# A new written order for the side work of two state-space layers: 99 parts of a block, placed anew among its 16 steps

## The chip, the cores and the metric

The kernel runs on one core of a Trainium2 chip. The metric is device time in microseconds (us), the median of several executions. One execution is also recorded by the hardware profiler; its span, from the first to the last instruction, and its rows are what is read here.

## What is computed

The input x has 64 sequences of 64 tokens with 256 features, and each sequence has a condition vector of 512. Four layers are added to x in turn: two conditioned attention layers (L0, L1; 16 heads) and two state-space layers (L2, L3). The change touches only the state-space layers. Cut to what matters, one of them is:

```python
xr, gate = split(x @ W_in.T, 2)              # 512 + 512 features
xc = silu(conv(xr + t_emb, W_conv) + b_conv) # four taps along the sequence, each feature alone
xn = layernorm(xc) * ln_g + ln_b
Bm, Cm, dt = split(xn @ W_xproj.T, 3)        # 16 states
dt = tanh(dt @ W_dt.T + b_dt) * 0.01
Ad = 1 + dt * -tanh(A_log)
Bd = Bm * minimum(norm(xn), 1)
h  = clip(h * Ad + Bd * xn, -10, 10)         # one step; h is 16 x 512 for each sequence
y  = Cm . h + D * xn
x  = x + (y * silu(gate)) @ W_out.T
```

Everything is fp32.

## The kernel before

The attention layers come first. The two state-space layers are then cut into 16 **blocks** (`items`, L150): 2 layers x 2 groups of 32 sequences x 4 pieces of 16 tokens. A block has 16 **steps** of the recurrence, so there are 256 steps in a row, and a step works on all 32 sequences: 8 sequences x 16 states fill the 128 partitions, in four groups of 512 columns.

What makes up step i is written at the end of the kernel (L1064 to L1118), with a moment for each part:

- `clips(i)` at i: two instructions of VectorE (DVE), one for each half of the state, which add the scaled state `v` to the input products `pu`, bound the sum and write `h`.
- `scales(i+1, half)` at i + 0.2 and i + 0.3: four instructions of ScalarE (ACT), two for each half, `v` = `h` times the decay of the next step.
- `inputs(i+1)` at i + 0.5: four products of TensorE (PE) into `pu`, from the spread weights `bd` and the normalized `xn`. Each half of `pu` has one buffer, so a half is written only after its clip.
- `outputs` of two steps together, at the odd step + 0.6: eight products into `py`.

All other work of a block is **side work**: 99 parts, methods of `Block` (L153 to L515). In the order of a block they are: for each of four feature groups c, `project` (PE, the input projection), `collect` (ACT copies it, GpSimd, POOL, adds the condition), `begin` and three `tap`s (ACT, then DVE: the convolution), `silu` (ACT); for each of four token groups j, `turn_x` (PE transposes), `stats` (DVE, two small POOL operations, DVE), `norm` (POOL) and `length` (ACT); once, `shared`, `keep`, `flip`, `flipped`, `params`, `decay`, `spreads`, `turn_a`, `turned_a`, `turn_c`, `turned_c`, `strength`, `by_step` (the parameters of the recurrence); `spread_b` (POOL, the weights `bd` of four steps); `gate` (PE, two products for each c) and `open` (ACT); `skip` (POOL) and `take` (DVE: y from `py`); `turn_y` (PE) and `gated` (DVE); `leave` (PE, eight products of the output projection, accumulated for two halves oc) and `residual` (DVE; in the second layer also the stores on the SP queue).

Where each part goes is written out in a table, `plan` (L996 to L1028): a moment in steps, counted from the block's first step. A part at -34.951 of block n is issued 34.951 steps before block n starts, so among the steps of block n - 3. Moments of all blocks, and those of the steps, are sorted (L1116), and the parts are issued in that order. Each engine instruction is pinned to it (`pin`, L104), so each engine works its own instructions in exactly this order; it waits in front of the first one whose operands or buffers are not ready. Parts that the attention phase already did for blocks 0 to 2 are left out (`done`), the last block has an `ending` of its own (L1030), and five steps of preparation for the second layer's weights are put at 9.15 to 13.15 (L1053).

Buffers bear on it too. PSUM has eight banks here: two halves of `pu` with two banks each, one for `py`, one for `acc` (the projection), and two **side banks** (`side_bank`, L142) that all other products share: `turn_x`, `shared`, `flip`, `turn_a`, `turn_c`, the gates, `turn_y` and the two sums of `leave`. A gate's bank is held from its first product to `open`, a sum's from its first `leave` to its `residual`.

Of the kernel before, what the change touches and what calls it, by code (L numbers as in the profile page):

```python
# [60 lines left out]
def tile_kernel(ctx: ExitStack, tc: tile.TileContext, ins, out):  # L61
# [916 lines left out]
    with tc.tile_pool(name="m1", bufs=1) as m1, tc.tile_pool(  # L978
# [6 lines left out]
        for i in range(2):  # L985
# [8 lines left out]


        plan = [  # L996
            (-34.951, "project", 0), (-34.145, "collect", 0), (-32.918, "begin", 0),
            (-32.296, "tap", 0, 1), (-32.249, "tap", 0, 2), (-31.945, "tap", 0, 3),
            (-31.244, "silu", 0), (-30.886, "project", 1), (-29.870, "collect", 1),
            (-28.982, "begin", 1), (-28.108, "tap", 1, 1), (-28.033, "tap", 1, 2),  # L1000
            (-27.458, "tap", 1, 3), (-27.391, "silu", 1), (-27.108, "project", 2),
            (-25.727, "collect", 2), (-25.628, "begin", 2), (-24.258, "tap", 2, 1),
            (-24.257, "tap", 2, 2), (-23.560, "tap", 2, 3), (-23.559, "silu", 2),
            (-23.297, "project", 3), (-22.516, "collect", 3), (-21.680, "begin", 3),
            (-20.388, "tap", 3, 1), (-20.387, "tap", 3, 2), (-19.648, "tap", 3, 3),
            (-19.425, "silu", 3), (-18.608, "turn_x", 0), (-17.021, "stats", 0),
            (-14.414, "turn_x", 1), (-13.823, "stats", 1), (-13.037, "norm", 1),
            (-12.466, "length", 1), (-11.619, "turn_x", 2), (-10.326, "stats", 2),
            (-9.009, "shared"), (-8.837, "keep"), (-8.735, "flip"), (-8.734, "flipped"),
            (-8.314, "turn_x", 3), (-7.276, "norm", 0), (-7.023, "norm", 2), (-7.022, "length", 2),  # L1010
            (-6.528, "stats", 3), (-5.896, "length", 0), (-4.945, "norm", 3), (-4.663, "params"),
            (-3.934, "decay"), (-3.655, "spreads"), (-3.160, "turn_a"), (-2.843, "turned_a"),
            (-1.863, "length", 3), (-1.855, "strength"), (-1.854, "by_step"),
            (-1.719, "spread_b", 0), (-1.036, "gate", 0, 0), (-0.523, "gate", 0, 1),
            (-0.416, "spread_b", 2), (-0.078, "open", 0), (0.962, "turn_c"), (1.060, "turned_c"),
            (1.971, "spread_b", 1), (2.598, "gate", 1, 1), (2.842, "gate", 2, 0),
            (3.137, "gate", 1, 0), (3.278, "open", 1), (3.495, "skip", 0), (4.308, "take", 0),
            (4.595, "gate", 2, 1), (4.863, "open", 2), (5.711, "spread_b", 3), (7.365, "skip", 1),
            (8.657, "take", 1), (10.567, "skip", 3), (12.293, "skip", 2), (13.392, "take", 2),
            (14.025, "gate", 3, 1), (14.668, "gate", 3, 0), (15.371, "open", 3),  # L1020
            (16.062, "turn_y", 1), (16.607, "gated", 1), (16.957, "turn_y", 0),
            (17.151, "gated", 0), (17.536, "take", 3), (22.035, "turn_y", 3),
            (22.093, "turn_y", 2), (22.428, "gated", 3), (22.838, "gated", 2),
            (23.084, "leave", 0, 3), (24.583, "leave", 0, 2), (26.250, "leave", 1, 2),
            (27.268, "leave", 1, 1), (27.476, "leave", 1, 0), (27.494, "leave", 1, 3),
            (28.056, "leave", 0, 1), (28.309, "residual", 1), (28.898, "leave", 0, 0),
            (29.565, "residual", 0),
        ]  # L1028

        ending = [  # L1030
# [150 lines left out]
```

## Time and profile before

| | us |
|---|---|
| median of 3 runs | 1613.23 (1610.12 to 1615.07) |
| the profiled execution: time | 1610.09 |
| its span | 1608.3 |
| attention, up to the first clip of the scan | 0 to 579.1 |
| 256 steps, first clip's start to last clip's end | 579.1 to 1597.3 |
| a block of 16 steps, between blocks 2 and 12 | 63.6 to 63.9 |
| block 0, 13, 14 | 66.6, 62.2, 62.2 |

In the profile PE is TensorE, PEld its weight loads, DVE VectorE, ACT ScalarE, POOL GpSimd and SP the engine that issues the DMAs. A row of groups gives line, engine, operation, out<-in with shapes and count, then the busy time in us and the mean of one instruction in ns, then how long the engine stood idle before them and what ended that. A row of the timeline gives the start in us, the length, the engine, the operation and, in brackets, the idle time before it. An fp32 matmul appears as two instructions, so `pu` of one step counts x8. Its ends are modelled: successive rows overlap a little, and the distance from one start to the next says better how long something held the engine.

### The profile page before, as it was taken

To read this page: it belongs to the slowest core of one execution; us is meant where nothing else is said; L and a number is where in the kernel's file an instruction comes from. 1 tells how busy PE (TensorE), PEld (TensorE's weight loads), DVE (VectorE), ACT (ScalarE), POOL (GpSimd) and SP (SyncE) were. 2 spreads that over 40 slices of the span, in tenths; PEclk is the share of its full clock that TensorE was granted. 3 is DMA by queue.
4 is the path that set the end of the run, shared out by engine and by line. 5 is a ranking of instruction groups with operands and counts; after the bars stand their busy time and mean duration, and the time that the engine had idled before them with its cause. 6 is when DMAs were issued, how large, how long until landed. Compare 5 with 4: busy or idle time off the path is not lost. (4 is left out here: it accounts for less than half of the span.)

```text
span 1608.3 us, 30098 instructions
## 1 busy us (share of the span) xinstructions
PE 1525.1 (95%) x12352; PEld 661.3 (41%) x12352; DVE 1304.2 (81%) x1480; ACT 1122.1 (70%) x1899; POOL 868.6 (54%) x862
## 2 busy tenths in 40 slices
PE   5899999999999688999999999999999999999888
PEld 2555555555555333333333333333333333333323
DVE  3777677777767687989989989889899899898775
ACT  3555555455456477888878888888888887887774
POOL 2467666646667656455455464554564644645420
PEclk9999999999999889999999999999999999999999
DMA  7000000000000010000000000000000000000001
GB/s 240 2 2 2 2 2 1 2 2 2 1 2 2 1 64 1 1 1 1 1 1 1 1 1 1 0 1 1 1 1 14 14 1 14 14 1 14 9 5 27
DMA packets 19337, 18.26 MB, mean 11 GB/s; under 512 B 5472, under 2 KB 16352, under 8 KB 19200
## 3 DMA queue, kind: packets, MB, share of 16 engines
q1 hardware_dynamic: 19200, 16.34, 3.2%
q8 instruction: 98, 1.61, 0.4%
q14 instruction: 39, 0.32, 0.1%
HBM read 12.14 MB, written 4.19 MB: 10 GB/s over the span
## 5 line engine op out<-in xcount | busy, mean ns | idle before, releaser
L113 ACT ACTIVATE v<-h,ad 128x512 f32<-128x512 f32 x1008 | 649.6, 711 | 142.3 <-DVE h L1082 133.9
L1082 DVE CUSTOM_DVE_ANT_0 h<-v,pu 128x1024 f32<-128x1024 f32 x504 | 592.3, 1216 | 111.2 <-ACT v L113 51.5
L107 PE MATMUL pu<-xn,bd 32*128 32x512 f32 x2048 | 293.6, 641 | 35.0 <-DVE h L1082 31.3
L107 PE MATMUL py<-h,cd 128*32 128x512 f32 x2048 | 247.1, 600 | 0.1
L107 PE MATMUL pw<-xm,aw 128*128 128x512 f32 x384 | 179.6, 606 | 3.9 <-POOL xm L730 3.9
L206 POOL TENSOR_TENSOR xr<-xr,cT 128x512 f32<-128x512 f32 x55 | 70.6, 1283 | 194.6 <-ACT xr L205 194.6
L107 PEld LDWEIGHTS pu<-xn,bd 32*128 32x128 f32 x2048 | 83.3, 183 | 177.0 <-issue 139.8
L822 POOL TENSOR_TENSOR pr<-pr,sm 128x1024 f32<-128x1024 f32 x64 | 121.1, 1903 | 21.7 <-DVE sm L821 20.2
L306 POOL TENSOR_SCALAR mv<-mv 128x1 f32<-128x1 f32 x64 | 14.7, 230 | 214.2 <-DVE mv L304 212.9
L107 PE MATMUL pg<-xt,win 128*128 128x512 f32 x256 | 126.8, 617 | 0.0
L107 PE MATMUL pw<-z,wo 128*128 128x512 f32 x240 | 126.6, 630 | 0.0
L117 DVE SCALAR_TENSOR_TENSOR acc<-xr,cv,acc 128x512 f32<-128x512 f32 x165 | 123.8, 751 | 2.0
L107 PE MATMUL acc<-xt,win 128*128 128x512 f32 x256 | 124.4, 609 | 0.7 <-ACT xc L113 0.7
L107 PEld LDWEIGHTS py<-h,cd 128*32 128x32 f32 x2048 | 53.7, 109 | 165.6 <-issue 163.0
L836 ACT COPY pT<-pt 128x512 f32<-128x512 f32 x128 | 68.4, 586 | 76.1 <-PE pt L110 76.1
L113 ACT ACTIVATE pr<-pr 128x1024 f32<-128x1024 f32 x64 | 67.7, 1057 | 61.1 <-DVE pr L123 61.1
L107 PEld LDWEIGHTS pw<-xm,aw 128*128 128x128 f32 x384 | 68.9, 191 | 74.0 <-issue 65.3
L440 POOL TENSOR_TENSOR dx<-xn,rep 128x512 f32<-128x512 f32 x64 | 82.0, 1281 | 18.7 <-DVE ys L123 18.7
L718 POOL TENSOR_TENSOR sq<-sq 128x512 f32<-128x512 f32 x16 | 20.4, 1277 | 129.2 <-ACT sq L113 129.2
L811 DVE TENSOR_REDUCE mx<-ps 128x16 f32<-128x1024 f32 x64 | 78.3, 1223 | 13.7 <-PE ps L107 13.7
L323 POOL TENSOR_TENSOR xn<-xg,rep 128x512 f32<-128x512 f32 x64 | 81.7, 1277 | 8.0 <-ACT xg L113 3.3
L123 DVE TENSOR_TENSOR pr<-ps,mx 128x1024 f32<-128x1024 f32 x64 | 78.4, 1225 | 8.6 <-DVE mx L811 0.5
(150 smaller groups left out, 2324.9 us busy)
## 6 DMA issues: line engine op xcount, KB each, us to landing
xt<-in_xT SPq DMA_DIRECT2D x8, 512.0 KB, 7.8
out_xT<-xt SPq DMA_DIRECT2D x14, 256.0 KB, 2.3
aw<-in_aw SPq DMA_DIRECT2D x10, 256.0 KB, 6.3
win<-in_win SPq DMA_DIRECT2D x2, 1024.0 KB, 8.3
rep<-in_rep SPq DMA_DIRECT2D x2, 784.0 KB, 7.7
wo<-in_wo SPq DMA_DIRECT2D x2, 512.0 KB, 8.0
out_xT<-xt SPq DMA_DIRECT2D x2, 192.0 KB, 2.5
wx<-in_wx SPq DMA_DIRECT2D x2, 96.0 KB, 7.2
```

Source lines behind the costliest of these rows:

```text
L107: pin(nc.tensor.matmul(*args, **kw))
L113: pin(nc.scalar.activation(*args, **kw))
L117: nc.vector.scalar_tensor_tensor(out=out, in0=in0, scalar=scalar, in1=in1, op0=op0, op1=op1)
L123: pin(nc.vector.tensor_tensor(*args))
L206: pin(nc.gpsimd.tensor_tensor(curb, curb, bc(temb, 2, BT), ALU.add))
L323: pin(nc.gpsimd.tensor_tensor(self.xn[j], xg, self.rep[:, DI : 2 * DI], ALU.add))
L440: pin(nc.gpsimd.tensor_tensor(self.dx[j], self.xn[j], self.rep[:, 2 * DI : 3 * DI], ALU.mult))
L718: pin(nc.gpsimd.tensor_tensor(a, a, self.sq[:, 1, :], ALU.add))
L811: pin(nc.vector.tensor_reduce(mx, s4, AX.X, ALU.max))
L822: pin(nc.gpsimd.tensor_tensor(pr, pr, bc(sm, 3, S), ALU.mult))
L836: pin(nc.scalar.copy(self.pT[g][:, c, :, :], pt))
L1082: nc.vector._custom_dve(TENSOR_ADD_SAT, out=hn, in0=vs.pop((i, h)), in1=pu[h], s0=10.0, s1=-10.0)
```

## The change

Only the table `plan` is replaced; its 99 parts stay the same, and no other line differs. Moments move by up to some ten steps. Where two neighbouring parts keep their order between the parts of the steps, nothing changes on an engine; where they do not, its list changes.

```diff
         plan = [
-            (-34.951, "project", 0), (-34.145, "collect", 0), (-32.918, "begin", 0),
-            (-32.296, "tap", 0, 1), (-32.249, "tap", 0, 2), (-31.945, "tap", 0, 3),
-            (-31.244, "silu", 0), (-30.886, "project", 1), (-29.870, "collect", 1),
-            (-28.982, "begin", 1), (-28.108, "tap", 1, 1), (-28.033, "tap", 1, 2),
-            (-27.458, "tap", 1, 3), (-27.391, "silu", 1), (-27.108, "project", 2),
-            (-25.727, "collect", 2), (-25.628, "begin", 2), (-24.258, "tap", 2, 1),
-            (-24.257, "tap", 2, 2), (-23.560, "tap", 2, 3), (-23.559, "silu", 2),
-            (-23.297, "project", 3), (-22.516, "collect", 3), (-21.680, "begin", 3),
-            (-20.388, "tap", 3, 1), (-20.387, "tap", 3, 2), (-19.648, "tap", 3, 3),
-            (-19.425, "silu", 3), (-18.608, "turn_x", 0), (-17.021, "stats", 0),
-            (-14.414, "turn_x", 1), (-13.823, "stats", 1), (-13.037, "norm", 1),
-            (-12.466, "length", 1), (-11.619, "turn_x", 2), (-10.326, "stats", 2),
-            (-9.009, "shared"), (-8.837, "keep"), (-8.735, "flip"), (-8.734, "flipped"),
-            (-8.314, "turn_x", 3), (-7.276, "norm", 0), (-7.023, "norm", 2), (-7.022, "length", 2),
-            (-6.528, "stats", 3), (-5.896, "length", 0), (-4.945, "norm", 3), (-4.663, "params"),
-            (-3.934, "decay"), (-3.655, "spreads"), (-3.160, "turn_a"), (-2.843, "turned_a"),
-            (-1.863, "length", 3), (-1.855, "strength"), (-1.854, "by_step"),
-            (-1.719, "spread_b", 0), (-1.036, "gate", 0, 0), (-0.523, "gate", 0, 1),
-            (-0.416, "spread_b", 2), (-0.078, "open", 0), (0.962, "turn_c"), (1.060, "turned_c"),
-            (1.971, "spread_b", 1), (2.598, "gate", 1, 1), (2.842, "gate", 2, 0),
-            (3.137, "gate", 1, 0), (3.278, "open", 1), (3.495, "skip", 0), (4.308, "take", 0),
-            (4.595, "gate", 2, 1), (4.863, "open", 2), (5.711, "spread_b", 3), (7.365, "skip", 1),
-            (8.657, "take", 1), (10.567, "skip", 3), (12.293, "skip", 2), (13.392, "take", 2),
-            (14.025, "gate", 3, 1), (14.668, "gate", 3, 0), (15.371, "open", 3),
-            (16.062, "turn_y", 1), (16.607, "gated", 1), (16.957, "turn_y", 0),
-            (17.151, "gated", 0), (17.536, "take", 3), (22.035, "turn_y", 3),
-            (22.093, "turn_y", 2), (22.428, "gated", 3), (22.838, "gated", 2),
-            (23.084, "leave", 0, 3), (24.583, "leave", 0, 2), (26.250, "leave", 1, 2),
-            (27.268, "leave", 1, 1), (27.476, "leave", 1, 0), (27.494, "leave", 1, 3),
-            (28.056, "leave", 0, 1), (28.309, "residual", 1), (28.898, "leave", 0, 0),
-            (29.565, "residual", 0),
+            (-34.879, "project", 0), (-34.720, "collect", 0), (-34.633, "begin", 0),
+            (-33.762, "tap", 0, 1), (-32.894, "tap", 0, 2), (-32.566, "tap", 0, 3),
+            (-32.565, "silu", 0), (-31.236, "project", 1), (-30.916, "collect", 1),
+            (-30.065, "begin", 1), (-28.224, "tap", 1, 1), (-28.223, "tap", 1, 2),
+            (-27.735, "tap", 1, 3), (-27.425, "silu", 1), (-26.834, "project", 2),
+            (-26.461, "collect", 2), (-25.058, "begin", 2), (-24.473, "tap", 2, 1),
+            (-24.064, "tap", 2, 2), (-23.845, "tap", 2, 3), (-23.358, "silu", 2),
+            (-23.074, "project", 3), (-22.756, "collect", 3), (-22.104, "begin", 3),
+            (-21.929, "tap", 3, 1), (-20.282, "tap", 3, 2), (-19.380, "tap", 3, 3),
+            (-19.357, "silu", 3), (-18.968, "turn_x", 0), (-18.058, "stats", 0),
+            (-14.435, "turn_x", 1), (-13.645, "stats", 1), (-11.623, "turn_x", 2),
+            (-10.897, "norm", 0), (-10.812, "length", 0), (-10.053, "stats", 2),
+            (-10.052, "norm", 2), (-9.499, "shared"), (-8.665, "keep"), (-8.250, "turn_x", 3),
+            (-7.092, "length", 2), (-6.345, "stats", 3), (-5.989, "flip"), (-5.825, "flipped"),
+            (-5.824, "params"), (-5.686, "decay"), (-5.144, "spreads"), (-4.236, "turn_a"),
+            (-3.382, "norm", 3), (-3.306, "turned_a"), (-3.276, "norm", 1), (-2.841, "length", 3),
+            (-1.920, "length", 1), (-0.646, "strength"), (-0.637, "by_step"),
+            (-0.636, "spread_b", 0), (-0.636, "spread_b", 1), (-0.635, "gate", 0, 1),
+            (0.558, "turn_c"), (0.559, "turned_c"), (1.526, "gate", 0, 0), (2.256, "open", 0),
+            (2.853, "gate", 1, 1), (2.912, "skip", 0), (3.191, "gate", 2, 1),
+            (3.200, "gate", 1, 0), (3.213, "spread_b", 2), (3.639, "open", 1), (4.278, "take", 0),
+            (4.417, "spread_b", 3), (5.088, "gate", 2, 0), (5.088, "open", 2), (8.209, "skip", 1),
+            (8.511, "skip", 2), (8.597, "take", 1), (12.046, "skip", 3), (12.174, "take", 2),
+            (14.587, "gate", 3, 1), (14.790, "gate", 3, 0), (15.873, "open", 3),
+            (16.070, "turn_y", 1), (16.545, "gated", 1), (17.046, "take", 3),
+            (17.476, "turn_y", 0), (17.477, "gated", 0), (22.325, "turn_y", 2),
+            (22.326, "gated", 2), (22.364, "turn_y", 3), (22.381, "gated", 3),
+            (23.280, "leave", 0, 0), (24.804, "leave", 0, 3), (26.021, "leave", 0, 2),
+            (26.537, "leave", 0, 1), (26.574, "leave", 1, 2), (27.053, "leave", 1, 0),
+            (27.632, "residual", 0), (28.514, "leave", 1, 1), (29.637, "leave", 1, 3),
+            (30.996, "residual", 1),
         ]
```

Sorted by engine, and modulo 16 steps, the products of PE between the input products of step k and those of step k + 1 (a part with a moment from k - 0.5 to k + 0.5) differ as follows; even k also hold the outputs of two steps:

| k | before | after |
|---|---|---|
| 1 | turn_y 0, turn_c, project 1 | turn_c, project 1, turn_y 0 |
| 2 | turn_x 1 | gate (0,0), turn_x 1 |
| 7 | shared, leave, flip | shared, leave |
| 10 | leave | flip, leave |
| 12 | leave | turn_a |
| 13 | turn_a, leave, project 0, turn_x 0 | leave, turn_x 0, project 0 |
| 14 | gate (3,1) | leave |
| 15 | gates (3,0), (0,0), (0,1) | gates (3,1), (3,0), (0,1) |

The other k hold the same kinds and numbers of products before and after.

## Prediction

> **What bounds the kernel now.** I read the page's busy shares and groups first, then the busy time by stage, then the timeline of the tensor engine. The page: busiest is PE, and the two costliest groups are the scales on ACT and the clips on DVE, each of which waits for the other and for the input products `pu`.
>
> ```profile
> PE 1525.1 (95%) x12352; PEld 661.3 (41%) x12352; DVE 1304.2 (81%) x1480; ACT 1122.1 (70%) x1899; POOL 868.6 (54%) x862
> L1082 DVE CUSTOM_DVE_ANT_0 h<-v,pu 128x1024 f32<-128x1024 f32 x504 | 592.3, 1216 | 111.2 <-ACT v L113 51.5 <-PE pu L107 49.8 <-issue 3.2
> L107 PE MATMUL pu<-xn,bd 32*128 32x512 f32 x2048 | 293.6, 641 | 35.0 <-DVE h L1082 31.3 <-DVE h L1079 2.9 <-ACT ad L113 0.4
> ```
>
> Busy time by stage, for a stretch inside the state-space steps (length, then PE, PEld, DVE, ACT, POOL busy): PE is at 98, DVE at 92, ACT at 85.
>
> ```profile
> 900.00:1000.00 100.00, 97.82 (x592) 35.94 (x588) 92.04 (x106) 84.61 (x147) 48.68 (x57) 1.00 0.00 1
> ```
>
> So a step has a floor, and PE fills most steps to it. The floor is seen late in the scan, where little else runs (timeline of all engines):
>
> ```profile
> 1561.60 2.35 DVE L1082 CUSTOM_DVE_ANT_0 h<-v,pu 128x1024 f32<-128x1024 f32 x2 [0.37 <-ACT v L113]
> ...
> 1564.10 1.14 PE L107 MATMUL pu<-xn,bd 32*128 32x512 f32 x8 [1.62 <-DVE h L1082]
> ...
> 1565.41 1.22 DVE L1082 CUSTOM_DVE_ANT_0 h<-v,pu 128x1024 f32<-128x1024 f32 x1 [1.46 <-ACT v L113]
> ```
>
> Two clips 2.35, 0.15 until the next input products may overwrite their banks, 1.14 for these, 0.17 to the next clip: 3.81 to 3.83 us. I call what PE does between the input products of step k and those of step k+1 **slot k** (k from 0 to 15 in a block). From the PE timeline, start to start, in the slot of step 13:
>
> ```profile
> 822.67 1.14 PE L107 MATMUL pu<-xn,bd 32*128 32x512 f32 x8
> 823.74 1.07 PE L107 MATMUL pa<-const,exa 128*128 128x16 f32 x8
> 824.66 1.10 PE L107 MATMUL pw<-z,wo 128*128 128x512 f32 x2
> 825.60 1.88 PE L107 MATMUL acc<-xt,win 128*128 128x512 f32 x4
> 827.32 0.60 PE L110 MATMUL ptr<-const,xc 128*128 128x128 f32 x4
> 827.85 1.14 PE L107 MATMUL pu<-xn,bd 32*128 32x512 f32 x8
> 828.92 1.92 PE L107 MATMUL py<-h,cd 128*32 128x512 f32 x16
> 830.77 1.12 PE L107 MATMUL pg<-xt,win 128*128 128x512 f32 x2
> 831.83 1.14 PE L107 MATMUL pu<-xn,bd 32*128 32x512 f32 x8
> ```
>
> The products stand without a gap: 1.07 + 0.92 + 0.94 + 1.72 + 0.53 = 5.18 us for step 13, and 1.07 + 1.85 + 1.06 = 3.98 for step 14. PE idles where the slot holds too little, as in step 4:
>
> ```profile
> 788.42 1.92 PE L107 MATMUL py<-h,cd 128*32 128x512 f32 x16
> 790.28 0.66 PE L110 MATMUL ptr<-const,xc 128*128 128x128 f32 x4
> 791.18 1.14 PE L107 MATMUL pu<-xn,bd 32*128 32x512 f32 x8 [0.24 <-DVE h L1082]
> ```
>
> Read so over the block that starts at 773 us, the steps 0 to 15 last, from input products to input products, 3.83 3.83 3.82 3.87 3.83 3.84 3.95 4.22 3.83 3.85 3.98 3.84 3.98 5.18 3.98 3.84: 63.67 us. PE's idle in it is four gaps of 0.24 to 0.25 (steps 0, 2, 4, 8), 0.98 us; 62.7 is products, which no order removes. That is the whole prize: 0.98 us a block, some 15 of 1608.
>
> **The change part by part.** No instruction is added or removed; every one is issued in the written order, so only slots differ. Prices, start to start, from the same timeline: a product pair of 512 columns 0.96 (1.06 straight before `pu`), three of them 2.77 to 2.80, a projection 1.72 to 1.83, a turn of x or y 0.50 to 0.59, `shared` 1.88, `flip` 0.31, `turn_a` 0.92, `turn_c` 0.44, the outputs of two steps 1.85, `pu` 1.07.
>
> - Slot 13 loses `turn_a` (to slot 12): 1.07 + 0.96 + 0.56 + 1.83 = 4.42. `turn_x` 0 now follows `turn_a` into a PSUM bank that ACT's `turned_a` must empty behind `silu` 3 and the scales: these end 0.1 before step 13's clip, plus 0.57 and 0.31 is 0.8 after it, where PE arrives at 0.7. Between 0 and 0.16; I take 0.1. Step 13: 4.52 instead of 5.18.
> - Slot 12 has `turn_a` for a leave: 1.07 + 1.85 + about 1.0 = 3.92 (was 3.98).
> - Slot 7 loses `flip`: 1.07 + 1.88 + 1.05 = 4.00 (was 4.22). Slot 10 gains it: 1.07 + 1.85 + 0.31 + 1.05 = 4.28 (was 3.98).
> - Slot 2 gains the gate product of (0, 0): 1.07 + 0.96 + 0.56 + 1.85 = 4.44 (was 3.82, with 0.24 idle). Slot 15 has the second product of gate 3 for it, and stays three products; slot 14 has a leave for the gate: 3.98 both.
> - Slots 3, 5, 6, 9, 11 keep number and kind; slots 0, 4, 8 keep their idle. In slot 1 the turn is last: 2.69 to 2.76, floor 3.83.
>
> After: 3.83 3.83 4.44 3.87 3.83 3.84 3.95 4.00 3.83 3.85 4.28 3.84 3.92 4.52 3.98 3.84 = **63.65 us** against 63.67. The crest of step 13 is spread, but it was work and not waiting.
>
> Costed at nothing, with the cover: the DVE moves (`take` 2 from step 13 to 12, residuals to 11 and 14, the first tap of c = 3 to step 10) leave at most 2.35 + 1.6 a step, below PE's 3.84 to 4.5 nearly everywhere, as before (a step with `stats` takes 3.88 to 3.95 already; if PE did not cover it, that is the 0.1 such a step would cost). On ACT `collect` 1 comes ahead of step 2's scales and waits for its projection: scales 0.15 late, covered by slot 2's 4.44; without that cover 0.15 a block. POOL (about 51 busy in 100) has the same rows; `strength` to the first `spread_b` is 0.24 + 1.04 + 0.29 + 0.61 + 1.06 + gaps, 3.6 us behind the last `length`, and ends about 0.5 before `pu` needs it. SP's stores leave with the residuals, one two steps earlier, one later; nothing waits for them.
>
> The ends. Blocks 13 and 14 have no projections of later blocks. Before, that emptied slot 13 to the floor (62.2 a block, measured from clip to clip); now slots 2 and 10 keep their excess (63.65 less 4.52, plus 3.83, is 62.96): +0.7 each. In block 15 a bank is missing at step 12 now, because both output sums are open:
>
> ```profile
> 1580.65 1.92 PE L107 MATMUL py<-h,cd 128*32 128x512 f32 x16
> 1584.00 0.63 PE L110 MATMUL pyt<-const,ys 128*128 128x128 f32 x4 [1.43 <-DVE xt L123]
> ```
>
> With the first residual at step 11 this wait goes (5.84 to 3.83); what is late next is slot 14 with a leave more and the second residual on DVE ahead of the last clip (3.77 to 4.6): -2.0 + 0.8 = -1.2. In block 0 step 2 and the scales behind `collect` 1 cost +0.8, scales behind the copy for layer 1 in step 10 +0.7, and step 13 loses its wait for `exa` (5.62 to 3.9; -1.7, `turn_a` +0.1): -0.1; block 1 -0.2.
>
> Sum: 11 blocks x -0.02 = -0.2, +1.4, -1.2, -0.3: **-0.3 us**. Against the profiled execution (span 1608.3, time 1610.1, so 1.8 lie around the span) that is 1609.8; the median shown, 1613.2, lies 3.1 above that execution, so 1613 for a median.
>
> **The rivals.** A measurement of this kernel can tell about 0.3%, 4.8 us, from no change.
>
> 1. Slower: **ACT's list in steps 12 to 14 runs late.** Between the scales of steps 13 and 15 stand `silu` 3, `turned_a`, `length` 3, `collect` 0, `begin` 0, `length` 1: 0.57 + 0.31 + 0.81 + 0.56 + 0.77 + 0.81 = 3.83 us (before, 3.02 spread over one step more), with two waits inside: `collect` 0 for a projection that ends last in slot 13 (about 0.5), and `begin` 0 for POOL's 1.28 (0.1). With eight scales at 0.64 that is 9.55, in the 9.7 until the second clip of step 15 wants its operand. From 0.15 us of lateness on, each further one holds the clips, and through `strength` the weights of the next block's first `pu`. For it: it is the tightest place, with three engines in a ring. Against it: ACT's rows overlap (four scales of 0.71 take 2.56), so the list may take 3.4. At 0.85 us late it costs 0.7 x 13 = 9: 1622. Chance 0.28.
> 2. Faster: **the remaining gaps of PE close.** For it: slot 2's is filled. Against it: slots 0, 4 and 8 hold what they held. All four closed give 0.98 x 13 = 13 us: 1600; half of them is about where it could be told from no change. Chance 0.12.
> 3. Faster: **PE's products do not bind**, and with the crest gone each step falls to the floor: 16 x 3.83 = 61.3, 2.4 x 13 = 31 us less: 1582. Against it: steps 7, 13 and 14 last as long as their products. Chance 0.03. The Trainium skill (Perfetto Trace Analysis, Identifying the Most-Contended Engine) speaks for this rival: matmul busy time is no measure of how near the engine is to its limit, and the weight loads' share is to be used. That share is 36 in 100 here. By that rule there is room and the time would be this rival's; the row of step 13, where four kinds of product add up to the step without a gap, speaks against it.
>
> That the order stays what it was is no rival: every engine's list is pinned as issued.
>
> **How the numbers follow.** Same, 0.57, at 1613; slower 0.28; faster 0.12 + 0.03. The main case alone: 1609 to 1618 (turn_x's wait 0 or 0.16, ends +-2, and the median's own scatter, 1610 to 1615). The range for 8 in 10 reaches down to 1605, into rival 2, and up to 1623, past rival 1's 1622; the rest is left out on both sides.
>
> **What would show it.** Right: step 13 at about 4.5, step 2 at 4.4, step 10 at 4.3, step 7 at 4.0, the block at 63.6 to 63.8, PE at 98 in 100; blocks 13 and 14 longer, block 15 shorter, step 12 of the last block near 3.8. Wrong for rival 1: clips of steps 14 to 16 waiting for ACT, or `pu` for `bd`. Wrong for my whole reading: a block whose PE idle is far from 1 us, or steps below the sum of their products.

## The result, and the profile after

The changed kernel takes 1607.0 us (median of 8 runs, 1603.8 to 1608.8), the kernel before 1612.3 us (8 runs beside them, 1610.1 to 1615.5): a ratio of 0.9964, 95% interval 0.9954 to 0.9975. That is 5.3 us less, some 0.36%, just past the 0.3% that the prediction took as the border of "same"; the interval reaches across that border. The forecast was 1613, with 1605 to 1623 as range; its main case alone was 1609 to 1618.

The page of the changed kernel, same rows as before: PE's share is the same, and the clips wait 12 us less in all (99.0, where it was 111.2); about half of it still ends with the scales `v` from ACT.

```profile
PE 1521.2 (95%) x12352; PEld 659.3 (41%) x12352; DVE 1307.4 (82%) x1480; ACT 1122.4 (70%) x1899; POOL 867.1 (54%) x862
L1082 DVE CUSTOM_DVE_ANT_0 h<-v,pu 128x1024 f32<-128x1024 f32 x504 | 594.0, 1217 | 99.0 <-ACT v L113 50.4
L107 PE MATMUL pu<-xn,bd 32*128 32x512 f32 x2048 | 292.8, 640 | 34.8 <-DVE h L1082 30.2
```

Busy time by stage of the changed kernel, the stretch that was shown before: again PE 98, DVE 92, ACT 84 of 100.

```profile
900.00:1000.00 100.00, 98.12 (x582) 36.33 (x584) 91.79 (x105) 84.41 (x147) 48.40 (x56) 1.00 0.00 1
```

The time by stretches, from the clips' starts in the two profiled executions (us):

| | before | after | difference | predicted |
|---|---|---|---|---|
| up to the first clip | 579.1 | 579.1 | 0 | 0 |
| blocks 0 and 1 | 130.6 | 129.6 | -1.0 | -0.3 |
| blocks 2 to 12 | 700.6 | 696.1 | -4.6 | -0.2 |
| blocks 13 and 14 | 124.5 | 125.4 | +0.9 | +1.4 |
| block 15 to the end | 73.6 | 72.2 | -1.4 | -1.2 |

So the ends came out about as worked out, and what was missed is 0.4 us in each full block. From input products to input products, in the block that starts at 772 us:

| step | 0 | 1 | 2 | 3 | 4 | 5 | 6 | 7 | 8 | 9 | 10 | 11 | 12 | 13 | 14 | 15 | block |
|---|---|---|---|---|---|---|---|---|---|---|---|---|---|---|---|---|---|
| before | 3.83 | 3.83 | 3.82 | 3.87 | 3.83 | 3.84 | 3.95 | 4.22 | 3.83 | 3.85 | 3.98 | 3.84 | 3.98 | 5.18 | 3.98 | 3.84 | 63.67 |
| predicted | 3.83 | 3.83 | 4.44 | 3.87 | 3.83 | 3.84 | 3.95 | 4.00 | 3.83 | 3.85 | 4.28 | 3.84 | 3.92 | 4.52 | 3.98 | 3.84 | 63.65 |
| after | 3.84 | 3.81 | 4.42 | 3.84 | 3.84 | 3.84 | 3.95 | 4.00 | 3.84 | 3.84 | 4.16 | 3.84 | 3.92 | 4.28 | 3.98 | 3.84 | 63.24 |

Fourteen of the sixteen steps are within 0.03 of the prediction. PE's timeline of the changed kernel in slot 13, the first that is not:

```profile
822.84 1.12 PE L107 MATMUL pw<-z,wo 128*128 128x512 f32 x2
823.80 0.60 PE L110 MATMUL ptr<-const,xc 128*128 128x128 f32 x4
824.24 1.88 PE L107 MATMUL acc<-xt,win 128*128 128x512 f32 x4
826.05 1.14 PE L107 MATMUL pu<-xn,bd 32*128 32x512 f32 x8
```

A leave 0.96, turn_x 0.44, the projection 1.81: the turn did not wait for its bank (ACT's `turned_a` ended 0.11 ahead of it), and it is 0.12 cheaper than the 0.56 that I put in. Slot 10, the second:

```profile
812.78 0.44 PE L110 MATMUL pxt<-const,sp 128*128 128x128 f32 x2
813.05 1.02 PE L107 MATMUL pw<-z,wo 128*128 128x512 f32 x2
814.01 1.14 PE L107 MATMUL pu<-xn,bd 32*128 32x512 f32 x8
```

The flip is 0.27, not 0.31, and the leave behind it 0.96, not 1.05. Slot 2 holds gate, turn and outputs without a gap, as predicted:

```profile
778.28 1.14 PE L107 MATMUL pu<-xn,bd 32*128 32x512 f32 x8
779.35 1.12 PE L107 MATMUL pg<-xt,win 128*128 128x512 f32 x2
780.31 0.60 PE L110 MATMUL ptr<-const,xc 128*128 128x128 f32 x4
780.84 1.92 PE L107 MATMUL py<-h,cd 128*32 128x512 f32 x16
782.70 1.14 PE L107 MATMUL pu<-xn,bd 32*128 32x512 f32 x8
```

And in the last block the turn of step 12 no longer waits for a bank (timeline of the changed kernel): it stands 1.86 behind the start of the outputs, where it stood 3.35 behind.

```profile
1576.14 1.92 PE L107 MATMUL py<-h,cd 128*32 128x512 f32 x16
...
1578.00 0.66 PE L110 MATMUL pyt<-const,ys 128*128 128x128 f32 x4
```

### The profile page after: what moved, and what is told of

Read it like the earlier page. It is cut to its first block, busy times and chain, and to the rows that moved or that the text cites. A ratio compares the mean times of both kernels' runs of the same rounds, so it can differ in the third digit from the quotient of the medians.

```text
span 1602.4 us, 30143 instructions
## 1 busy us (share of the span) xinstructions
PE 1521.2 (95%) x12352; PEld 659.3 (41%) x12352; DVE 1307.4 (82%) x1480; ACT 1122.4 (70%) x1899; POOL 867.1 (54%) x862
## 5 line engine op out<-in xcount | busy, mean ns | idle before, releaser
L123 DVE TENSOR_TENSOR t<-pw,dc 128x512 f32<-128x512 f32 x64 | 44.2, 691 | 44.6 <-PE pw L107 43.5
```

Source lines behind the costliest of these rows:

```text
L123: pin(nc.vector.tensor_tensor(*args))
```

## The experiments

**Theory 1**: a step is the longer of the 3.83 floor and the sum of its products on PE; the order can win only idle PE time (step 2's gap) and the prices that products have beside each other. **Theory 2**: what paid is that the crest of step 13 (5.20 us) was cut. A block's length from the trace tells more than single times: seven of the eleven blocks 2 to 12 agree to 0.01 us, before and after, while the stretch up to the first clip alone took 579.1 to 583.8 us in the profiled executions of the runs. The length is given from clip to clip (before 63.68, after 63.24).

### gate_back: the crest stays cut, step 2 gets its gap back

```diff
-            (1.526, "gate", 0, 0),
+            (-0.634, "gate", 0, 0),
```

> The new table with one product, the gate of (0,0), put back from the slot of step 2 into that of step 15 (moment -0.634), all else as in the new table, so step 13 stays at 4.28 us. Theory 1 (a step is the longer of 3.83 and the sum of its products on PE, and the new table gains because step 2's idle PE time got a product): step 15 rises from 3.84 to about 4.77, step 2 falls from 4.42 only to the floor 3.83, or to 4.1 if the scales behind collect 1, which come 0.2 late in step 1, lose the cover of slot 2; the block goes from 63.24 to 63.6 - 63.85, so most or all of the 0.44 us that a block gained is lost and the time is within 0.2% of the kernel before. Theory 2 (what paid is that the crest of step 13 is cut): step 13 is still cut, so the block stays within 0.1 us of 63.24 and the time 0.3% below the kernel before.

Measured: 1614.0 us, ratio to the kernel before 1.0009 (0.9999 to 1.0018); the block 63.81. PE's timeline of this run, slot 15 and then slot 2:

```profile
895.52 1.14 PE L107 MATMUL pu<-xn,bd 32*128 32x512 f32 x8
896.59 3.70 PE L107 MATMUL pg<-xt,win 128*128 128x512 f32 x8
900.22 1.14 PE L107 MATMUL pu<-xn,bd 32*128 32x512 f32 x8
```

```profile
845.15 0.66 PE L110 MATMUL ptr<-const,xc 128*128 128x128 f32 x4
845.74 1.92 PE L107 MATMUL py<-h,cd 128*32 128x512 f32 x16
848.17 1.14 PE L107 MATMUL pu<-xn,bd 32*128 32x512 f32 x8 [0.51 <-DVE h L1083]
```

Slot 15 has four products in a row (4.70 for the step), slot 2 idles 0.51: the gap of 0.25 and the late scales, now without cover. Step 13 is still 4.28, yet the block is 0.57 longer, more than the 0.44 that the table had won. Not all of that is the idle slot: the next run puts 0.25 of it on the late scales, and step 15 has become a new, smaller crest. So this run speaks against theory 2, and flip_moved and the added transposes below test it without these two effects.

### gate_back_collect: the wait that slot 2 covered

```diff
-            (-30.916, "collect", 1),
+            (-30.650, "collect", 1),
```

(on top of gate_back)

> As the run before, with collect 1 issued behind the scales of step 2 (moment -30.65) instead of ahead of them. It measures the wait that slot 2 covered. Theory 1: step 1 falls from 4.03 to 3.83 between clips, and the block is 0.2 to 0.27 us shorter than in the run with the gate alone, about 63.58. If the wait of the scales for collect 1 was no limit even without cover, the block is the same as in that run within 0.05 us.

Measured (one run, 1623.2 us): steps 1 and 2 together 7.75 instead of 8.00, the 0.25 expected. But the block is 64.35, 0.54 longer: step 3 rose from 3.82 to 4.61. ACT's timeline:

```profile
850.45 0.56 ACT L205 COPY xr<-acc 128x512 f32<-128x512 f32 x1
852.40 0.78 ACT L113 ACTIVATE acc<-xr,cv 128x512 f32<-128x512 f32 x1 [1.39 <-POOL xr L206]
```

`begin` 1 now follows `collect` 1 at once, and ACT stands 1.39 us until POOL has added the condition; the scales of step 3 stand behind it. My expectation missed this. It is the ring of ACT and POOL that rival 1 of the prediction named, at another step; in the changed kernel itself, scales between the two parts hide POOL's 1.28 us.

### one_product: the table before with one product carried to step 2

```diff
-            (14.025, "gate", 3, 1), (15.371, "open", 3), (-1.036, "gate", 0, 0), (-0.078, "open", 0),
-            (28.898, "leave", 0, 0), (29.565, "residual", 0),
+            (14.600, "gate", 3, 1), (15.873, "open", 3), (1.526, "gate", 0, 0), (2.256, "open", 0),
+            (29.637, "leave", 0, 0), (30.996, "residual", 0),
```

> The table before with the fewest moves that carry one product from the crest of step 13 to the slot of step 2: the last leave of (0,0) to step 14, gate (3,1) to step 15, gate (0,0) to step 2, with residual 0 and the two opens that depend on them; flip, turn_a, turn_x 0, taps, takes and norms stay as before. Theory 1: step 13 5.18 to 4.24, step 2 3.83 to 4.42, the block from 63.67 to 63.3 - 63.4, so most of the gain of the new table: 0.3% faster than the kernel before, within 0.1% of the new table. If the gain came from the other moves (flip to step 10, turn_a to step 12, the new order on DVE, ACT and POOL), the block stays at 63.6 or above.

Measured: 1683.6 us, ratio 1.0444 (1.0428 to 1.0460). Step 13 fell to 4.34 (4.24 expected) and step 2 rose to 4.41 (4.42 expected), but step 1 rose to 8.30 us. The timeline of slot 1:

```profile
791.97 0.68 DVE L123 TENSOR_TENSOR z<-pyt,z 128x512 f32<-128x512 f32 x1
...
792.71 0.66 PE L110 MATMUL pc<-const,exc 128*128 128x128 f32 x4 [2.48 <-DVE z L123]
```

PE waits 2.48 us for DVE's `gated` 0, which frees the only side bank that is left, since the gate's sum holds the other from step 15 to step 2. The wait is not the whole loss. PE's timeline behind it, and then the row of busy times for the stretch from 794.0 to 797.4 us:

```profile
793.20 2.88 PE L107 MATMUL acc<-xt,win 128*128 128x512 f32 x4
796.01 1.78 PE L107 MATMUL pu<-xn,bd 32*128 32x512 f32 x8
797.72 1.12 PE L107 MATMUL pg<-xt,win 128*128 128x512 f32 x2
```

```profile
794.00:797.40 3.40, 3.40 (x11) 0.85 (x9) 0.00 (x0) 2.91 (x5) 0.42 (x1) 0.51 0.00 0
```

The third number from the end is the granted clock, 0.51. Under it the projection takes 2.81 from start to start and `pu` 1.71, where the kernel before has 1.83 and 1.07 in this slot: 1.6 us more. The other blocks repeat it (0.50 from 862.3 to 865.6 us).

### one_product_bank: the order of slot 1 as in the new table

```diff
-            (0.962, "turn_c"), (1.060, "turned_c"), (16.957, "turn_y", 0), (17.151, "gated", 0), (17.536, "take", 3),
+            (0.558, "turn_c"), (0.559, "turned_c"), (17.476, "turn_y", 0), (17.477, "gated", 0), (17.046, "take", 3),
```

(on top of one_product)

> The run one_product lost 4.5 us in step 1 of each block (8.30 from clip to clip), where it was to gain. Reading: since gate (0,0) stands in step 2, gate (0,1) holds one of the two side banks of PSUM from step 15 to step 2, so turn_y 1, turn_y 0 and turn_c share the other one, and turn_c, behind turn_y 0 in PE's list, waits for gated 0 that DVE does after the clips of step 1. This run is one_product with the order of slot 1 as in the new table: turn_c, turned_c, then turn_y 0, gated 0 behind take 3. By this reading step 1 falls from 8.30 to 3.8 - 4.1 and the block from 68.29 to about 64.0; step 14 stays at 4.48 (stats 0 and residual 0 on DVE in one step), so it stays above the 63.67 of the table before. If the bank is not the cause, step 1 stays above 6.

Measured (one run, 1639.5 us): step 1 fell from 8.30 to 5.38, not to 4; the block 65.38, not 64.0. The wait for the bank, with the low clock behind it, was the larger part: from 709 to 1400 us the granted clock is 1.00 here. The rest is in this timeline:

```profile
787.25 0.60 ACT L113 ACTIVATE xc<-acc 128x512 f32<-128x512 f32 x1
...
787.91 1.98 PE L107 MATMUL acc<-xt,win 128*128 128x512 f32 x4 [1.18 <-ACT xc L113]
```

The projection waits 1.18 us for `silu` 0 to empty its one bank, and on ACT `silu` 0 now stands behind `turned_c`. In the new table `silu` 0 has moved to step 15, out of the way. So these few moves do not bring the gain: `turn_c` has to move too, and by these rows `silu` 0 and, on DVE, `stats` 0 or residual 0 (step 14 is 4.48 here). The table before with all of these moved was not run.

### flip_moved: a crest cut without a gap filled

```diff
-            (-8.735, "flip"), (-8.734, "flipped"), (28.056, "leave", 0, 1), (26.250, "leave", 1, 2),
+            (-5.989, "flip"), (-5.825, "flipped"), (26.250, "leave", 0, 1), (27.800, "leave", 1, 2),
```

(in the table before)

> The table before with flip and flipped moved from step 7 to step 10 as in the new table; for the PSUM bank that it needs there two leaves change places (0,1 to step 10, 1,2 to step 12). Nothing else moves. Theory 1: the sum of products is the same, so step 7 falls from 4.22 to 4.00, step 10 rises from 3.98 to 4.16 - 4.28, and the block is within 0.1 us of 63.67. Theory 2 (a lower crest pays): step 7's crest of 4.25 between clips is gone, 0.2 us less a block.

Measured: step 7 from 4.25 to 4.00, step 10 from 3.88 to 4.06 between clips, the block 63.63 instead of 63.68. A cut crest gave 0.05, not theory 2's 0.2. (One run, 1614.3 us; its block 0 has a step of 9.5 us, of which more below.)

### more_in_idle_slot and more_in_full_slot: does PE bind?

Two transposes are issued twice, with the same values, in slot 4 and in slot 1:

```diff
+            for c in range(2) if j == 2 else ():      # turn_x
+                tr(self.ptr[j][:, c * P : (c + 1) * P], self.xc[c][:, j * P : (j + 1) * P], ident)
```

```diff
+            for c in range(2) if j == 0 else ():      # turn_y
+                tr(self.pyt[j][:, c, :], ys[:, c * P : (c + 1) * P], ident)
```

> The new table with two of the four transposes of turn_x 2 done twice (the same values again), in the slot of step 4, where PE idles 0.25 us. Two transposes are 0.22 - 0.27 us on PE. Theory 1 (PE's products bind only where they fill the step): hidden, step 4 at 3.83 - 3.87 between clips, block 63.24 + 0.05 at most.

> The new table with two of the four transposes of turn_y 0 done twice, in the slot of step 1, where PE has no idle time but the clips of step 2 wait for ACT's scales (4.03 from clip to clip) and not for PE. Theory 1: PE has no gap until the end of slot 2, so the block grows by the full 0.22 - 0.27 us, to 63.5. If the products do not bind and the scales set steps 1 and 2, it grows by 0.05 or less, as in the other run.

Measured (one run each): the block 63.24 with more in slot 4, as without, and 63.46 with more in slot 1, 0.22 longer. The whole times, 1609.2 and 1609.1 us, do not show this, since the stretch up to the first clip differs by 2.6 us between the two. PE's timeline of the first, six transposes for four, and the idle 0.25 ahead of `pu` gone from the row:

```profile
857.70 0.87 PE L110 MATMUL ptr<-const,xc 128*128 128x128 f32 x6
858.61 1.14 PE L107 MATMUL pu<-xn,bd 32*128 32x512 f32 x8
```

The same work costs nothing where PE idles and its full length where it does not, even in a step whose clips wait for the scales, because PE has no gap until the end of slot 2.

### gaps_filled: pieces of products for the idle slots

Gate (0,0) is split in halves of 256 columns and leave (0,2) into 192 and 320 columns (`gate` and `leave` take a range):

```diff
-            (1.526, "gate", 0, 0), (26.021, "leave", 0, 2),
+            (0.080, "gate", 0, 0, 0, 2), (1.526, "gate", 0, 0, 2, 4),
+            (24.100, "leave", 0, 2, 0, 192), (26.021, "leave", 0, 2, 192, 512),
```

> The new table with two products split by columns, so that a piece fits an idle slot: half of gate (0,0) goes from slot 2 to slot 0, and 192 of the 512 columns of leave (0,2) from slot 10 to slot 8. Theory 1 (idle PE time in a block is what can be won): step 2 from 4.42 to about 3.97, step 10 from 4.16 to 3.85, steps 0 and 8 at 3.83 - 3.95, less some 0.05 - 0.1 for each further product: the block from 63.24 to 62.7 - 62.95, 4 to 6 us in all. If the idle 0.25 us of slots 0 and 8 cannot be used, the block stays at 63.2 or above.

Measured: the block 62.84, the time 1599.1 us, ratio to the kernel before 0.9917 (0.9900 to 0.9935). In slot 0 the half gate fills the gap:

```profile
835.89 0.66 PE L110 MATMUL pyt<-const,ys 128*128 128x128 f32 x4
836.38 0.60 PE L107 MATMUL pg<-xt,win 128*128 128x256 f32 x2
836.91 1.14 PE L107 MATMUL pu<-xn,bd 32*128 32x512 f32 x8
```

Two gaps filled give 0.40 a block, as theory 1 has it.

### first_half_first: the gaps removed at the floor

```diff
-            for g in (2, 3, 0, 1):
+            for g in (0, 1, 2, 3):
```

> The new table, with the four input products of a step issued for state half 0 first (groups 0, 1, 2, 3 instead of 2, 3, 0, 1). Half 0 is clipped first, so its two products need not wait for the second clip. Theory 1: in full slots nothing changes; in the slots of steps 0, 4, 8, where PE idles, the first two can start up to 0.25 us earlier. If two of them alone take half of the 1.07 us, the idle 0.76 us of a block goes and it falls to about 62.5 (0.6% faster than the new table); if two alone take nearly as long as four together, the steps 0, 4, 8 get longer by 0.2 - 0.5 each. I hold the second for likelier, since the four stand as one run of 1.07 for eight instructions where a single product of 512 columns takes 0.96: they run side by side.

Measured: the block 62.80, the time 1593.2 us, ratio 0.9882 (0.9865 to 0.9898). Steps 0, 4 and 8 fell from 3.80 - 3.83 to 3.51 - 3.53. Of my two cases I held the wrong one for likelier, though the gain is less than the 0.76 of the other. PE's timeline of slot 4:

```profile
789.39 0.66 PE L110 MATMUL ptr<-const,xc 128*128 128x128 f32 x4
789.98 1.30 PE L107 MATMUL pu<-xn,bd 32*128 32x512 f32 x8
791.21 1.13 PE L107 MATMUL pg<-xt,win 128*128 128x512 f32 x2
```

No gap ahead of `pu`: the pair for half 0 goes early, and the four take 1.23 instead of 1.07. From the turn's start to the next slot it is 0.59 + 1.23 = 1.82 us; in the changed kernel it is 0.91 + 1.07 = 1.98. So two pairs apart cost 0.16 more than together, the start is 0.32 earlier, and 0.16 a slot is won. The emptier blocks 13 to 15 gain too: from block 13 to the end 123.3 + 69.6 = 192.9 us, against 125.4 + 72.2 = 197.6. This one-line edit on the new table is the fastest version run.

### single_ahead, and both together

```diff
-            (-4.236, "turn_a"), (29.637, "leave", 1, 3), (27.632, "residual", 0),
+            (-4.450, "turn_a"), (29.550, "leave", 1, 3), (27.530, "residual", 0),
```

> The new table with two parts moved by less than half a step, so that they stand ahead of the outputs py in their slots instead of straight before the input products: leave (1,3) in slot 14 and turn_a in slot 12 (residual 0 goes 0.1 ahead of turn_a for the bank). The same products in the same slots. A single product before pu takes 1.05 - 1.06 from start to start, before another kind of product 0.96. Theory 1 with neighbour prices: step 14 from 3.98 to 3.88, step 12 from 3.92 to 3.85, the block from 63.24 to 63.07, 2 us or 0.1% in all. Without neighbour prices: 63.24.

> The two edits of first_half_first and single_ahead together on the new table. If they add up, the block goes from 62.80 to about 62.63, the time to about 1591, 1.3% below the kernel before.

Measured: the block 63.65 with single_ahead, 0.41 longer instead of 0.17 shorter; 63.20 with both, so the two edits add up (62.80 + 0.40) with the wrong sign. Times 1611.1 us, ratio to the kernel before 0.9996 (0.9985 to 1.0007), and 1598.9 us, 0.9915 (0.9899 to 0.9931). The timeline of steps 12 and 13 shows where it went:

```profile
822.45 1.93 PE L107 MATMUL py<-h,cd 128*32 128x512 f32 x16
824.44 0.69 DVE L123 TENSOR_TENSOR ys<-py,dx 128x512 f32<-128x512 f32 x1 [0.37 <-PE py L107]
825.83 0.60 ACT L113 ACTIVATE xc<-acc 128x512 f32<-128x512 f32 x1 [0.30 <-DVE acc L117]
826.33 0.31 ACT L113 ACTIVATE ad<-pa,one 128x64 f32<-128x64 f32 x1
826.69 0.66 PE L110 MATMUL ptr<-const,xc 128*128 128x128 f32 x4 [0.19 <-ACT ad L113]
```

With `turn_a` first, the outputs end 1 us later; `take` 2 on DVE waits 0.37 for them, the last tap stands behind it, `silu` 3 on ACT waits 0.30 for that tap, `turned_a` stands behind `silu` 3, and turn_x 0 waits for the bank. And there was nothing to win: the leave straight ahead of `py` takes 1.06, as ahead of `pu`. The price falls on a single product between two of the tiled products (`pu` uses 32 rows, `py` 32 columns), whichever of them comes first.

### before_first_half: the same line in the table before

> The table before, with the four input products of a step issued for state half 0 first. In the new table that removed the gaps of slots 0, 4 and 8 at some 0.1 each for two pairs that no longer run side by side (63.24 to 62.80). Theory 1: the old table has one gap more (slot 2), so it gains more, 63.67 to about 63.1, and of the 0.43 us between the tables the part that was idle time, about 0.15, goes, while the part that was neighbours' prices stays: new minus old 0.3 a block instead of 0.43. If the gain of the change lay elsewhere, the two tables stay 0.43 apart.

Measured: the block 63.18, the time 1602.5 us, ratio 0.9937 (0.9914 to 0.9960). The tables stand 0.38 apart instead of 0.44; I had said 0.3. That does not decide. Each idle slot pays 0.16 for the split, and the old table has four where the new one has three. With the gap of slot 2 at 0.22, as the profile's idle column has it, theory 1 then gives 0.44 - 0.22 + 0.16 = 0.38; with the gap at 0.31 from start to start it gives 0.29. The slot of the old gap itself won 0.16 (outputs 1.85 and `pu` 1.23, for 2.17 and 1.07), which is the second count; but in the old table the three projections behind idle slots became 0.03 to 0.04 longer, and slot 4 won only 0.12, and why was not tried.

## Why the prediction was right or wrong

- **What bounds the kernel** was right, and is now shown: work added on PE costs its length in a full slot and nothing in an idle one. Rival 3 (products do not bind) falls with it. The rule of the Trainium skill that stood beside it (Perfetto Trace Analysis, Identifying the Most-Contended Engine) judges headroom by the share of weight loads, next to a count of operations; that share alone, 36 in 100, spoke for room. Here 0.22 us more of products made a block 0.22 longer.
- **"The crest of step 13 is spread, but it was work and not waiting"** was right: in flip_moved a cut crest gave 0.05, and in gate_back step 13 stayed cut while the gain went.
- **The step that failed is the sum of 63.65**, in the sizes of its terms, not in the mechanism. It was 0.41 too long: 0.24 in step 13 (the turn 0.44 instead of 0.56, its wait for the bank 0 instead of 0.1, the projection 1.81 instead of 1.83), 0.12 in step 10 (the flip 0.27 instead of 0.31, the leave 0.96 instead of 1.05) and 0.07 in steps 1 to 3, less 0.02 elsewhere. I had these prices as ranges (0.50 to 0.59 for a turn, 0.96 or 1.06 for a single product) and took them from places with other neighbours. A turn between two products of the full array took 0.44; single products between tiled ones, three before (slots 10, 12, 14), are two after (slots 7, 14). 0.41 a block over 11 blocks is 4.5 us, of the 5.7 by which the forecast misses the difference between the two profiled executions.
- **"62.7 is products, which no order removes"** was wrong. By the profile's idle column, PE's idle after the change is 0.76 (three gaps) and the products are 62.48, so 0.22 of the gain is the idle time of step 2 and 0.21 is products that got cheaper by their neighbours. From start to start the gap is larger: in slot 2 the outputs held PE for 2.17 until `pu`, and now for 1.85, so 0.31 or 0.32 is idle time and 0.12 is prices. The ends of rows are modelled, so the second count is the better one; both parts are there in either.
- **The idle time after the change** was put too high: the gaps in the sum (steps 0, 4, 8, 0.07 in step 1, 0.1 in step 13) came to 0.92, so I saw the gap of step 2 go and gave most of it back to waits that I assumed. Only the three gaps are there.
- **That the time lies in the range is in part luck**: 1607.0 is below the main case's 1609 to 1618, and the range reached down to 1605 only for rival 2, all of whose gaps would have had to close for 1600.
- **Rival 1 (ACT's list late in steps 12 to 14)** did not come: in the changed kernel the second half's scales end 0.36 to 0.49 ahead of the clips of steps 14 and 15. But the place is as tight as said: 1 us later outputs in single_ahead went through DVE and ACT into PE and cost 0.4 us a block.
- **Rival 2 (gaps close)** was priced at 0.98 a block for all four; one closed and gave 0.22 by that count (0.31 from start to start). That the other three can be closed too is shown by first_half_first, at 0.16 each for the split pairs.
- **What was costed at nothing** held: `collect` 1 ahead of the scales made them late (step 1 is 4.03 between clips), and slot 2 covered it; without the cover it costs 0.25 (gate_back_collect), where I had 0.15. POOL's chain to `bd` and the stores cost nothing: in blocks 2 to 12 of the changed kernel the trace shows no wait of PE but those of `pu` for the clips.
- **The ends** were right in sign and about in size (+0.9 and -1.4 for +1.4 and -1.2); blocks 0 and 1 gained 1.0 for 0.3.

## What to carry to other kernels

When an engine is full, ask two things of a new order: how much idle time of that engine it fills, and how much dearer or cheaper its instructions get beside their new neighbours; peaks that are work cost nothing here. Then ask whether buffers still come free in time: one_product lost 4.5 us in step 1 of each block behind a bank that one moved product held longer, some of it to the low clock that followed. Take the price of a short instruction from a row with the same neighbours on both sides. And before reordering at all, look at the floor: which half of a dependence is asked for first won as much again as the new table in a full block (0.44), and over twice as much in the whole time (1.18% for both, 0.36% for the table), because it also helps where little else runs.

## What the runs showed of the hardware

- An fp32 product of 512 columns holds the full array for 0.86 us from start to start between other products of the full array (two projections take 1.72), 0.96 with a product of 32 rows or 32 columns on one side, and 1.05 to 1.06 with one on both; three between such products take 2.77 and four 3.63, which is 0.86 each and 0.2 for the two ends. The Trainium skill (TensorEngine Tiling (Array Packing), Key Properties) says that changing the tiling mode drains the engine; the rows fit that, with about 0.1 us as its price at each end here. They show the price, not the drain.
- Four products of 32 rows each take 1.07 together and 1.23 when the second pair has to wait; I had expected a pair alone to take nearly as long as four.
- In two runs a wait of PE was followed by a low clock, and the step lost more than the wait. In one_product, behind the wait of 2.48 us, the granted clock was 0.51 for 3.4 us and the next products took 1.6 us longer, in block after block. In block 0 of flip_moved it was 0.66 between 635 and 645 us, behind a wait of 2 us for `exa`, and that step took 9.5 us, where the kernel before, at 1.00 in that stretch and with a wait of 1.2, took 5.6. In one_product_bank PE waits 1.18 in each of blocks 2 to 12, and the clock stays at 1.00 there. That the wait brings the clock down is likely by this, but no run varied the wait alone.
